# The MLP of the first eight tile rows, done by two between the turns of the second attention half

## The chip, the core and the metric

The kernel runs on one core of a Trainium2 chip. The metric is the device time of one execution in microseconds (us). The core has five engines with a queue each: PE (matrix products), DVE (vector), ACT (activations and copies), POOL (GpSimd) and SP, which here only issues DMAs. In the traces, PEld is the weight load of PE.

## What is computed

Four sequences of 1024 rows with 128 channels go through four residual blocks: sparse attention (16 heads of 8; a row sees the 32 rows up to itself and every 64th row before it), an MLP with weights of +1 and −1, a Mamba block over the sequence, and the same MLP again.

```python
x = x + attention(layernorm(x))            # window 32, stride 64, 16 heads
x = x + ffn(layernorm(x), k0, k1, k2, s0, s1, s2)
x = x + mamba(layernorm(x))
x = x + ffn(layernorm(x), k0, k1, k2, s0, s1, s2)

def ffn(x):                                # 128 -> 512 -> 512 -> 128
    h = concat([x, -x])
    h = relu(s0 * (h @ where(k0, 1, -1))) * 2
    h = relu(s1 * (h @ where(k1, 1, -1))) * 2
    return s2 * (h @ where(k2, 1, -1))
```

## The kernel before

The four sequences are kept as two pairs of batches, `xs[0]` and `xs[1]`, each 128 partitions (2 x 64 rows) by 16 tiles by 128 channels. A tile is thus 64 rows of two sequences at once; a group is four tiles, called by pair and number (0_0 is the first group of the first pair).

**Attention** (`attention`, L201 to L590) runs over 32 tiles, pair 0 then pair 1, in a loop of turns (L546). In turn `i` it does one stage each of several tiles: products of the strided keys for tile `i+1` (`product`, POOL), scores (`scores`, PE) for `i+1`, softmax for `i` (DVE, ACT), weights and strided values for `i-2` (`weights`, `strided`), values for `i-3`, the division for `i-4`, the output projection and the residual for `i-5`. The strided work grows with the tile's number in its pair, on DVE and POOL alike. Beside this, `prep_steps` (L274) norms and projects a group of four tiles, two steps a turn, for groups to come: `xn` (ACT), its transpose `tp` (PE), `xnT`, the products `pq`, `pk`, `pn`, and by DMA on SP the keys `kx` (16 small DMAs a group), and the values out to memory (`vd`) and back (`vr`). ACT spreads `vr` into `vb` (`spread_values`, L477), one quarter a turn. The keys and values of a pair stand in `kv` and `vS` (two buffers each, L270). PE's results of all these steps rotate through five PSUM banks (`spare`, L213).

Within the attention each engine keeps the order in which the program issues its instructions (`keep`, L593); what comes after it in the program is put in order by the scheduler, which may place it between these. The layer norm statistics of the first MLPs stand that way inside the attention on DVE (`st_fa`) and POOL (`rs_fa`) already.

**MLP weights** (L648 to L673): DVE makes `w0`, `w1`, `w2` from the loaded bits after the attention.

**MLP** (`mlp`, L682): for a group of four tiles, norm (`fxna`, ACT), transpose (`ftpa`, PE), split of the transposed values into a high part (ACT) and the rest (`fxnTa`, DVE), first product `pfa` (8 matmuls of 512 columns), relu again as a high part (ACT) and a rest (`h1a`, DVE), second product `pga` (32 matmuls), relu `h2a`, last product `pfoa`, residual on DVE. Work is cut into pieces by generators; two `lanes` (L1186) hold the MLPs of all groups: 0_0 and 0_1 first, then 0_2 and 0_3, and so on. The second lane's first MLP uses buffers of the scans (`in_scan_buffers`, L1180).

**Mamba** needs for its first unit the norm of groups 0_0 and 0_1 (`mamba_norm`, L846; `st_z`, `rs_z`, `mxn`, `mtp`, `mxnT`), then `mamba_pre_half` (L901: convolution `pc`, `px`, `pd`). Until it is ready, a loop (L1204) runs it and the lanes' MLPs by turns. Then `scans` (L1026) works through 128 units, each a pair of scans and a product on DVE (`hs`, `hc`), a product on POOL (`db`) and sums, while the remaining MLPs are fed in by pieces. The last MLPs close the kernel.

Of the kernel before, what the change touches and what calls it, by code (L numbers as in the profile page):

```python
# [16 lines left out]
F32 = mybir.dt.float32  # L17
# [3 lines left out]
F32R = mybir.dt.float32r  # L21
AF = mybir.ActivationFunctionType
ALU = mybir.AluOpType
# [3 lines left out]
P = 128  # L27
B, T, C = 4, 1024, 128
NP = B // 2
R = 64  # L30
NT = T // R
# [4 lines left out]
EPS = 1e-5  # L36
FF = 512
E, N, DC, DR = 256, 16, 4, 8
NH = E // P
CH = 512  # L40
# [3 lines left out]
def hybrid_kernel(ctx: ExitStack, tc: tile.TileContext, x, Wq, Wk, Wv, Wo, ln_g, ln_b, W_in, conv_w,  # L44
# [36 lines left out]
    xs = []  # L81
# [24 lines left out]
    def load_mlp():  # L106
        for t, k in ((k0s, k0), (k1s, k1), (k2s, k2)):
            nc.sync.dma_start(t, k.rearrange("(i p) f -> p i f", p=P))
        for i, s in enumerate((s0, s1, s2, res_scale)):
            nc.sync.dma_start(scal[:, i : i + 1], s.partition_broadcast(P))  # L110
# [87 lines left out]
            )  # L198


    def attention(actx):  # L201


# [68 lines left out]
        prep = {}  # L272

        def prep_steps(cc):  # L274

            bp, c = divmod(cc, NT // 4)
            yield
            xn = ap2.tile([P, 4, C], F32, name=f"xn{cc}", tag="xn")
            rs = norms.pop(cc)
            for i in range(4):  # L280
                sc.activation(
                    xn[:, i, :], xs[bp][:, 4 * c + i, :], AF.Identity, bias=rs[:, 1, i : i + 1],
                    scale=rs[:, 0, i : i + 1],
                )
            yield
            tp = spare(f"tp{cc}")
            for i in range(4):
                te.transpose(tp[:, i * P : (i + 1) * P], xn[:, i, :], ident)
            yield
            xnT = ap2.tile([P, CH], F32, name=f"xnT{cc}", tag="xnT")  # L290
            sc.copy(xnT, tp)
            yield
            pq, pk = spare(f"pq{cc}"), spare(f"pk{cc}")
            te.matmul(pk, wqkv[:, 1, :], xnT, start=True, stop=True)
            te.matmul(pq, wqkv[:, 0, :], xnT, start=True, stop=True)

            def project(i):
                pn = spare(f"pn{cc}_{i}")
                te.matmul(
                    pn[:, : 3 * C], xnT[:, i * P : (i + 1) * P], wqkv.rearrange("p i c -> p (i c)"),  # L300
                    start=True, stop=True,
                )
                return pn

            qs = ap2.tile([P, 4, C], F32, name=f"qs{cc}", tag="qs")

            def keep_rows(i, pn):
                m = 4 * c + i
                sc.copy(qs[:, i], pn[:, :C])
                sc.copy(kv[bp][:, m], pn[:, C : 3 * C])  # L310
                sc.copy(vS[bp][:, :, m], pn[:, 2 * C : 3 * C])

            yield
            kx = kxs[cc % 2]
            qT = ap2.tile([P, CH], F32, name=f"qT{cc}", tag="qT")
            if cc == 0:

                sc.copy(qT, pq)
                for t in range(4):
                    ve.tensor_tensor(  # L320
                        kx[:, t], pk[:, t * P : (t + 1) * P].unsqueeze(1).to_broadcast([P, HB, P]),
                        head_of.unsqueeze(2).to_broadcast([P, HB, P]), ALU.mult,
                    )
            else:
                kT = ap2.tile([P, CH], F32, name=f"kT{cc}", tag="kT")
                sc.copy(kT, pk)
                queues = (nc.sync, nc.gpsimd) if cc == 1 else (nc.sync,)
                for h in range(H):
                    rows = slice(h * HD, (h + 1) * HD)
                    queues[h % len(queues)].dma_start(  # L330
                        kx[rows, :, h % HB, :], kT[rows, :].rearrange("p (t x) -> p t x", t=4)
                    )
                sc.copy(qT, pq)
            prep[cc] = qT, kx
            for i0 in (0, 2):
# [12 lines left out]
            prep[cc] = qT, kx, qs, vr  # L348
# [189 lines left out]
            ve.tensor_add(xs[bp][:, m, :], xs[bp][:, m, :], psum.pop(("y", i))[:, :C])  # L538


        LEAD = 7

        starts = {(3 if cc == 1 else 4 * cc) - LEAD: cc for cc in range(len(tiles) // 4)}
        preps = []
        last = len(tiles)
        for i in range(-LEAD, last + 5):  # L546
            def at(k, stage):
                if 0 <= i + k < last:
                    stage(i + k)

            if i == -LEAD:
                weights_in()
            if i == 0:
# [24 lines left out]
            at(-4, turn_out)  # L578
            at(-3, values)
            at(-4, keep_out)  # L580
            for p in preps:
                next(p, None)
            cc, step = divmod(i + LEAD, 4)
            if cc + 2 < last // 4:
                stats(cc + 2, range(step, step + 1))
                if step == 3:
                    scales(cc + 2)
            cc, step = divmod(i + 1, 4)
            if 0 <= cc < last // 4:
                spread_values(cc, range(step, step + 1))  # L590

    with ExitStack() as actx:
        keep.append(True)  # L593
# [51 lines left out]
                    w.run()  # L645


    fw = ctx.enter_context(tc.tile_pool(name="ffnw", bufs=1))  # L648
    fx = ctx.enter_context(tc.tile_pool(name="ffnx", bufs=2))
    with tc.tile_pool(name="kload", bufs=1) as kl:  # L650


        sign = fw.tile([P, 2], F32, name="sign")
        below = fw.tile([P, 2], F32, name="below")
        ve.tensor_single_scalar(sign, scal[:, 0:2], 0.0, op=ALU.is_gt)
        ve.tensor_single_scalar(below, scal[:, 0:2], 0.0, op=ALU.is_lt)
        ve.tensor_sub(sign, sign, below)
        total = fw.tile([P, 1], F32, name="total")
        ve.tensor_mul(below, scal[:, 0:2], sign)
        ve.tensor_scalar_mul(below, below, 2.0)  # L660
        ve.tensor_mul(total, below[:, 0:1], below[:, 1:2])
        ve.tensor_mul(total, total, scal[:, 2:3])
        twice = fw.tile([P, 2], F32, name="twice")
        ve.tensor_scalar_mul(twice, sign, 2.0)

        w0 = fw.tile([P, FF], F32R, name="w0")
        diff = kl.tile([P, FF], F32, name="diff")
        ve.tensor_sub(diff, k0s[:, 0], k0s[:, 1])
        ve.tensor_scalar_mul(w0, diff, twice[:, 0:1])
        w1 = fw.tile([P, 4, FF], F32R, name="w1")  # L670
        ve.tensor_scalar(w1, k1s, twice[:, 1:2], sign[:, 1:2], ALU.mult, ALU.subtract)
        w2 = fw.tile([P, 4, C], F32R, name="w2")
        ve.tensor_scalar(w2, k2s, 2.0, -1.0, ALU.mult, ALU.add)  # L673
    waste = fw.tile([P, C], F32, name="waste")
    fed = set()

    CT = NT // 4
    HALF = CT // 2
# [501 lines left out]
    def in_scan_buffers(u):  # L1180

        return [m2.tile([P, 2, CH], F32R, name=f"h1{u}_{f}", tag="hc", bufs=6) for f in range(4)]
# [89 lines left out]
```

## Time and profile before

| what | us |
|---|---|
| median of 3 runs (929.16 to 929.56) | 929.18 |
| the profiled execution, whole | 928.12 |
| its span, first to last instruction | 926.3 |
| busy in the span: PE, DVE, POOL, ACT | 753.8, 772.2, 751.3, 588.9 |
| last residual of the attention (DVE) starts | 246.21 |
| first scan (`hs`) starts | 322.55 |

The span is what a trace shows; the difference of 1.8 us to the whole execution lies around it. Shares of busy time are means over very different stages. This is busy time in tenths in 40 slices of 23 us:

```profile
PE   5897578955698879968789988869889969778887
DVE  6799898999623378988799999899999999999952
ACT  4766447743436587788766887877868764754513
POOL 6799996999523287899888999989989998997921
```

The attention fills the first ten slices or so, the scans begin near the fourteenth.

### The profile page before, as it was taken

The page shows a single profiled execution, that of the slowest core. Times are in us where ns is not written, and L with a number is a line of the kernel's source. Part 1 is how long each engine was busy: PE and PEld are TensorE (multiplying, and loading weights), DVE is VectorE, ACT ScalarE, POOL GpSimd, SP SyncE. Part 2 cuts the span into 40 slices and gives each one's busy share as a digit, 9 for nine tenths or more (in the row PEclk, how much of TensorE's full clock was granted, in tenths as well). Part 3 has the DMA queues.
Part 4 walks back from the last instruction along what each step waited for, and adds up shares of the span by engine and source line. Part 5 has one row for each costly group of instructions (what it writes and reads, how often), then busy time and mean ns, then how long its engine had stood idle before and what let it go on. Part 6 is the DMA issues. An engine that isn't in the chain of part 4 may idle for free.

```text
span 926.3 us, 15255 instructions
## 1 busy us (share of the span) xinstructions
PE 753.8 (81%) x5628; PEld 454.6 (49%) x5628; DVE 772.2 (83%) x1033; ACT 588.9 (64%) x1292; POOL 751.3 (81%) x586
## 2 busy tenths in 40 slices
PE   5897578955698879968789988869889969778887
PEld 2454345533486544623346534536435626445556
DVE  6799898999623378988799999899999999999952
ACT  4766447743436587788766887877868764754513
POOL 6799996999523287899888999989989998997921
PEclk9899869996699977997999999999989989799998
DMA  4633313330100121112121121121221221222000
GB/s 134 118 71 68 61 18 69 72 63 2 42 6 1 47 69 47 49 66 67 48 70 46 69 70 47 68 70 46 80 70 46 80 81 46 80 68 73 30 23 12
DMA packets 47162, 53.09 MB, mean 57 GB/s; under 512 B 4824, under 2 KB 38400, under 8 KB 47088
## 3 DMA queue, kind: packets, MB, share of 16 engines
q1 hardware_dynamic: 45920, 51.59, 19.8%
q8 instruction: 44, 0.72, 0.3%
q0 software_dynamic: 608, 0.27, 0.2%
q10 hardware_dynamic: 560, 0.26, 0.1%
q14 instruction: 30, 0.25, 0.1%
HBM read 45.82 MB, written 4.46 MB: 54 GB/s over the span
## 4 chain that ended last, share of the span: by engine, by line
DVE 33%; PE 25%; ACT 16%; POOL 12%; issue 8%; SPq 3%; DMA 3%; DVEq 0%; POOLq 0%; ACTq 0%
DVE hs L57 16%; DVE hc L57 5%; ACT da L57 4%; PE pys L57 4%; PE pga L57 4%; POOL prod L57 3%; DVE S L57 3%; POOL prodv L57 3%; ACT L57 3%; PE pc L57 3%; SPq L330 2%; PE pfoa L57 2%; POOL db L57 2%; PE pd L57 2%; PE pgb L57 2%
## 5 line engine op out<-in xcount | busy, mean ns | idle before, releaser
L57 POOL TENSOR_TENSOR db<-du,bs 128x1024 f32<-128x1024 f32 x128 | 304.0, 2376 | 0.6 <-DMA bs<-bd 0.6
L57 ACT ACTIVATE da<-dt,a_t 128x512 f32<-128x512 f32 x256 | 175.5, 687 | 138.8 <-DVE hs L57 138.2
L57 POOL TENSOR_TENSOR hc<-hc,hc 128x512 f32<-128x512 f32 x128 | 163.9, 1281 | 51.3 <-DVE hc L57 51.3
L57 DVE TENSOR_TENSOR hc<-hs,pcc 128x1024 f32<-128x1024 f32 x128 | 155.9, 1218 | 23.5 <-PE pcc L57 15.6
L57 DVE TENSOR_TENSOR_SCAN hs<-da,db 128x512 f32<-128x512 f32 x128 | 149.0, 1205 | 12.5 <-POOL db L57 6.9
L57 DVE TENSOR_TENSOR_SCAN hs<-da,carry,db 128x512 f32<-128x512 f32 x128 | 156.9, 1266 | 1.9 <-ACT da L57 1.0
L57 PE MATMUL pys<-hc,ident 128*128 128x512 f32 x256 | 144.5, 650 | 0.1
L57 PE MATMUL pcc<-bc,spread 96*128 96x512 bf16 x128 | 52.8, 412 | 36.2 <-DVE hc L57 35.4
L57 PE MATMUL pga<-h1a,w 128*128 128x512 f32 x256 | 74.8, 442 | 8.1 <-ACT u L57 2.9
L57 PEld LDWEIGHTS pys<-hc,ident 128*128 128x128 f32 x256 | 51.7, 211 | 49.7 <-issue 23.6
L57 POOL TENSOR_TENSOR prodv<-vS,E 128x128 f32<-128x128 f32 (+14 forms) x30 | 69.7, 2322 | 5.8 <-ACT E L57 5.5
L57 POOL TENSOR_TENSOR prod<-kv,qs 128x128 f32<-128x128 f32 (+14 forms) x30 | 71.3, 2376 | 1.5 <-DVE or L57 1.4
L57 PEld LDWEIGHTS pga<-h1a,w 128*128 128x128 f32 x256 | 50.8, 202 | 30.7 <-issue 4.8
L57 ACT ACT_TABLE_LOAD x48 | 61.6, 1283 | 3.4 <-issue 2.6
L57 PE MATMUL pc<-mxnT,w_conv 128*128 128x512 f32 x128 | 60.8, 601 | 2.1 <-ACT gate L57 2.1
L57 PE MATMUL pgb<-h1b,w 128*128 128x512 f32 x192 | 56.9, 443 | 5.0 <-DVE h1b L57 3.9
L57 ACT ACTIVATE E<-S 128x512 f32<-128x512 f32 (+15 forms) x62 | 26.5, 473 | 52.4 <-DVE S L57 52.2
L57 PE MATMUL ps<-kx,qT 64*32 64x256 f32 x1008 | 46.5, 438 | 6.4 <-DVE S L57 5.5
L57 PE MATMUL py<-woT,oT 128*128 128x128 f32 x64 | 17.7, 363 | 40.2 <-ACT oT L57 39.9
L57 POOL TENSOR_TENSOR ep<-ep,eo 128x512 f32<-128x512 f32 x32 | 41.2, 1289 | 9.9 <-ACT ep L57 8.6
L57 PEld LDWEIGHTS pgb<-h1b,w 128*128 128x128 f32 x192 | 37.6, 197 | 23.0 <-issue 7.5
L57 ACT COPY ep<-pt 128x512 f32<-128x512 f32 x32 | 18.8, 587 | 38.5 <-DVE eo L57 36.6
(213 smaller groups left out, 1577.0 us busy)
## 6 DMA issues: line engine op xcount, KB each, us to landing
bs<-bd SPq DMA_DIRECT2D x64, 512.0 KB
vr<-vd SPq DMA_DIRECT2D x32, 256.0 KB
vd<-kv SPq DMA_DIRECT2D x8, 256.0 KB
x<-in_L_attn_a_x_dram SPq DMA_DIRECT2D x15, 128.0 KB
kx<-kT SPq DMA_DIRECT2D x104, 16.0 KB
out_dram<-x SPq DMA_DIRECT2D x12, 128.0 KB
taps<-in_L_attn_b_conv_w_dram SPq DMA_DIRECT2D x1, 512.0 KB
k1s<-in_L_ffn_k_dram SPq DMA_DIRECT2D x1, 256.0 KB
```

The source lines that it names most:

```text
L57: ins = getattr(self.engine, name)(*args, **kwargs)
L330: queues[h % len(queues)].dma_start(kx[rows, :, h % HB, :], kT[rows, :].rearrange("p (t x) -> p t x", t=4))
```

## The change

The MLP of groups 0_0 and 0_1 (eight tiles) leaves the lanes. A new generator `mlp_first` does it by two tiles, 256 columns at a time, in the attention's turns 17 and after; four calls of `other()` a turn advance it by one step each. It takes a buffer of `kv` and one of `vS`, those of pair 0, which are no longer needed then. Its PSUM banks come from `spare` too. The weights are made by `mlp_weights`, in turns 12 to 15, in parts. To make room for the weights, which now stand beside the attention's buffers, `xn`, `xnT` and `vr` have one buffer instead of two; `vr` is loaded two turns later and spread to `vb` by two quarters in a turn, two turns later; group 1's preparation starts one turn later. The scan buffers are no longer lent to the second lane.

```diff
+    def mlp_weights():
...
+        ve.tensor_single_scalar(sign, scal[:, 0:2], 0.0, op=ALU.is_gt)
...
+        yield
+        ve.tensor_sub(w0, k0s[:, 0], k0s[:, 1])
+        ve.tensor_scalar_mul(w0, w0.bitcast(F32), twice[:, 0:1])
+        ve.tensor_scalar(w2, k2s, 2.0, -1.0, ALU.mult, ALU.add)
+        for i in range(2):
+            yield
+            part = slice(2 * i, 2 * i + 2)
+            ve.tensor_scalar(w1[:, part], k1s[:, part], twice[:, 1:2], sign[:, 1:2], ALU.mult, ALU.subtract)
...
-            xn = ap2.tile([P, 4, C], F32, name=f"xn{cc}", tag="xn")
+            xn = ap2.tile([P, 4, C], F32, name=f"xn{cc}", tag="xn", bufs=1)
...
-            xnT = ap2.tile([P, CH], F32, name=f"xnT{cc}", tag="xnT")
+            xnT = ap2.tile([P, CH], F32, name=f"xnT{cc}", tag="xnT", bufs=1)
...
-            vr = ap2.tile([P, 16, C], F32, name=f"vr{cc}", tag="vr")
+            prep[cc] = qT, kx, qs
+            for _ in range(4):
+                yield
+            vr = ap2.tile([P, 16, C], F32, name=f"vr{cc}", tag="vr", bufs=1)
...
+        def mlp_first(nt):
+            cols = 2 * C
+            room = ap2.tile([P, NT * 2 * C], F32R, name="roomk", tag="kv")
+            rest = ap2.tile([P, C * NT], F32, name="roomv", tag="vS")
...
+            for t in range(nt):
+                if t % 2 == 0:
+                    yield
+                st = small.tile([P, 6], F32, tag="sta", name=f"stm{t}", bufs=2)
+                ve.bn_stats(st, xs[0][:, t, :])
+                ve.bn_aggr(mv[:, t, :], st)
+            yield
...
+            gp.tensor_tensor(rs[:, 0], rs[:, 0], minus_half[:, :nt], ALU.pow)
...
+            for t0 in range(0, nt, 2):
+                yield
+                for k in range(2):
...
+                    sc.activation(
+                        xn[:, k * C : (k + 1) * C], xs[0][:, t, :], AF.Identity, bias=rs[:, 1, t : t + 1],
+                        scale=rs[:, 0, t : t + 1],
+                    )
+                yield
+                tp = spare(f"mt{t0}")[:, :cols]
+                for k in range(2):
+                    te.transpose(tp[:, k * C : (k + 1) * C], xn[:, k * C : (k + 1) * C], ident)
+                yield
+                sc.copy(xnT[:, 0], tp)
+                yield
+                ve.tensor_sub(xnT[:, 1], tp, xnT[:, 0].bitcast(F32))
+                for f0 in (0, 2):
+                    yield
+                    pf = spare(f"mf{t0}_{f0}").rearrange("p (f c) -> p f c", f=2)
+                    for f in range(2):
+                        for s in range(2):
+                            te.matmul(
+                                pf[:, f], w0[:, (f0 + f) * P : (f0 + f + 1) * P], xnT[:, s], start=s == 0, stop=s == 1
+                            )
+                    yield
+                    sc.activation(h1[:, f0 : f0 + 2, 0], pf, AF.Relu)
+                    yield
+                    ve.scalar_tensor_tensor(
+                        h1[:, f0 : f0 + 2, 1], pf, 0.0, h1[:, f0 : f0 + 2, 0].bitcast(F32), ALU.max, ALU.subtract
+                    )
+                for f0 in (0, 2):
+                    yield
+                    pg = spare(f"mg{t0}_{f0}")
+                    for f in range(2):
+                        for j in range(4):
+                            for s in range(2):
+                                te.matmul(
+                                    pg[:, f * cols : (f + 1) * cols], w1[:, j, (f0 + f) * P : (f0 + f + 1) * P],
+                                    h1[:, j, s], start=j + s == 0, stop=j == 3 and s == 1,
+                                )
+                    yield
+                    sc.activation(h2[:, f0 * cols : (f0 + 2) * cols], pg, AF.Relu)
+                yield
+                po = spare(f"mo{t0}")[:, :cols]
...
+                yield
+                xc = xs[0][:, t0 : t0 + 2, :].rearrange("p m c -> p (m c)")
+                ve.scalar_tensor_tensor(xc, po, total, xc, ALU.mult, ALU.add)
...
-        starts = {(3 if cc == 1 else 4 * cc) - LEAD: cc for cc in range(len(tiles) // 4)}
+        starts = {4 * cc - LEAD: cc for cc in range(len(tiles) // 4)}
+        weights_made = mlp_weights()
+        beside = mlp_first(2 * NT // 4)
...
+            if NT - 4 <= i < NT:
+                next(weights_made, None)
+            def other():
+                if i > NT:
+                    next(beside, None)
...
             at(-2, weights_before)
+            other()
...
                 at(1, keep_scores)
+            other()
             at(0, softmax_scores)
             at(0, softmax_exp)
+            other()
...
             for p in preps:
                 next(p, None)
+            other()
...
-            cc, step = divmod(i + 1, 4)
-            if 0 <= cc < last // 4:
-                spread_values(cc, range(step, step + 1))
+            cc, step = divmod(i - 1, 4)
+            if 0 <= cc < last // 4 and step < 2:
+                spread_values(cc, range(2 * step, 2 * step + 2))
...
-    fed = set()
+    fed = {("a", 0, 0), ("a", 0, 1)}
...
-            early(0, lane, f1, lane, *[in_scan_buffers] * lane),
             early(0, 2 + lane, f1, lane),
```

On PE the new order in four turns of one pair of tiles is: transposes (`mt`) at the end of the first, then `mf` after the scores of the second and of the third, `mg` twice in the fourth (one before `py`, one after the scores), and `mo` in the next turn before `py`.

More of the change, by code (lines that the diff above doesn't have):

```diff
@@ L198, in ln_apply @@
             )
+    fw = ctx.enter_context(tc.tile_pool(name="ffnw", bufs=1))
+    w0 = fw.tile([P, FF], F32R, name="w0")
+    w1 = fw.tile([P, 4, FF], F32R, name="w1")
+    w2 = fw.tile([P, 4, C], F32R, name="w2")
+    total = fw.tile([P, 1], F32, name="total")
+    def mlp_weights():
+        sign = small.tile([P, 2], F32, name="sign", tag="sign", bufs=1)
+        below = small.tile([P, 2], F32, name="below", tag="below", bufs=1)
+        twice = small.tile([P, 2], F32, name="twice", tag="twice", bufs=1)
+        ve.tensor_single_scalar(sign, scal[:, 0:2], 0.0, op=ALU.is_gt)
+        ve.tensor_single_scalar(below, scal[:, 0:2], 0.0, op=ALU.is_lt)
+        ve.tensor_sub(sign, sign, below)
+        ve.tensor_mul(below, scal[:, 0:2], sign)
+        ve.tensor_scalar_mul(below, below, 2.0)
+        ve.tensor_mul(total, below[:, 0:1], below[:, 1:2])
+        ve.tensor_mul(total, total, scal[:, 2:3])
+        ve.tensor_scalar_mul(twice, sign, 2.0)
+        yield
[6 more added lines that the diff above has]
+            ve.tensor_scalar(w1[:, part], k1s[:, part], twice[:, 1:2], sign[:, 1:2], ALU.mult, ALU.subtract)
     def attention(actx):
@@ L538, in residual @@
             ve.tensor_add(xs[bp][:, m, :], xs[bp][:, m, :], psum.pop(("y", i))[:, :C])
+        def mlp_first(nt):
+            cols = 2 * C
+            room = ap2.tile([P, NT * 2 * C], F32R, name="roomk", tag="kv")
+            rest = ap2.tile([P, C * NT], F32, name="roomv", tag="vS")
+            h1 = room[:, : 8 * cols].rearrange("p (f s c) -> p f s c", f=4, s=2)
+            xnT = room[:, 8 * cols : 10 * cols].rearrange("p (s c) -> p s c", s=2)
+            h2, xn = rest[:, : 4 * cols], rest[:, 4 * cols : 5 * cols]
+            mv = small.tile([P, nt, 2], F32, name="mvm", tag="mvm", bufs=1)
+            for t in range(nt):
[5 more added lines that the diff above has]
+            yield
+            rs = small.tile([P, 2, nt], F32, name="rsm", tag="rsm", bufs=1)
+            gp.tensor_scalar_add(rs[:, 0], mv[:, :, 1], EPS)
+            gp.tensor_tensor(rs[:, 0], rs[:, 0], minus_half[:, :nt], ALU.pow)
+            gp.tensor_scalar_mul(rs[:, 1], mv[:, :, 0], -1.0)
+            gp.tensor_mul(rs[:, 1], rs[:, 1], rs[:, 0])
+            for t0 in range(0, nt, 2):
+                yield
+                for k in range(2):
+                    t = t0 + k
+                    sc.activation(
[38 more added lines that the diff above has]
+                po = spare(f"mo{t0}")[:, :cols]
+                for k in range(2):
+                    for f in range(4):
+                        te.matmul(
+                            po[:, k * C : (k + 1) * C], h2[:, f * cols + k * C : f * cols + (k + 1) * C],
+                            w2[:, f].bitcast(F32), start=f == 0, stop=f == 3,
+                        )
+                yield
+                xc = xs[0][:, t0 : t0 + 2, :].rearrange("p m c -> p (m c)")
+                ve.scalar_tensor_tensor(xc, po, total, xc, ALU.mult, ALU.add)
@@ L587, in attention @@
                     scales(cc + 2)
-            cc, step = divmod(i + 1, 4)
-            if 0 <= cc < last // 4:
-                spread_values(cc, range(step, step + 1))
+            cc, step = divmod(i - 1, 4)
+            if 0 <= cc < last // 4 and step < 2:
+                spread_values(cc, range(2 * step, 2 * step + 2))
+        for g in (weights_made, beside):
+            for _ in g:
+                pass
     with ExitStack() as actx:
@@ L645, in weave @@
                     w.run()
-    fw = ctx.enter_context(tc.tile_pool(name="ffnw", bufs=1))
     fx = ctx.enter_context(tc.tile_pool(name="ffnx", bufs=2))
[L650 to L674, printed above, removed]
-    fed = set()
+    waste = fx.tile([P, C], F32, name="waste", bufs=1)
+    fed = {("a", 0, 0), ("a", 0, 1)}
     CT = NT // 4
@@ L1178, in hybrid_kernel @@
     m2 = work.enter_context(tc.tile_pool(name="mam2", bufs=2))
-    def in_scan_buffers(u):
-        return [m2.tile([P, 2, CH], F32R, name=f"h1{u}_{f}", tag="hc", bufs=6) for f in range(4)]
     first_half = range(HALF)
```

## The prediction

> **What bounds the kernel now.** I read the page's 40 slices first, then busy time by stage, then the chain of waits over the stretch between attention and scans, then busy time turn by turn in the second half of the attention. Four stages come out: attention on the first pair of batches (up to 129.3 us), attention on the second pair (to 246.2), a stretch that gets the first scan going (to 322.5), and the scans with their tail.
>
> ```profile
> core 0: us, PE busy (x) PEld busy (x) DVE busy (x) ACT busy (x) POOL busy (x), PEclk, DMA share, GB/s
> 0.00:129.30 129.30, 93.13 (x1558) 55.49 (x1558) 108.37 (x241) 74.84 (x195) 112.42 (x108) 0.91 0.39 83
> 129.30:246.20 116.90, 86.04 (x1886) 57.29 (x1886) 104.88 (x188) 58.44 (x151) 100.90 (x63) 0.84 0.22 43
> 246.20:322.50 76.30, 67.48 (x294) 48.39 (x295) 27.69 (x66) 43.24 (x86) 22.20 (x35) 0.91 0.11 29
> 322.50:926.30 603.80, 507.13 (x1892) 293.44 (x1890) 531.24 (x538) 412.42 (x862) 515.73 (x382) 0.91 0.18 58
> ```
>
> In the third stage PE works 67.5 of 76.3 us while DVE and POOL, the two busiest engines of all other stages, rest for two thirds of it. The chain of waits says what PE does there (start, length, what):
>
> ```profile
> 255.38 3.75 PE pfa L57 x10
> 259.13 15.36 PE pga L57 x64
> 274.49 5.37 PE pfoa L57 x48
> ...
> 285.36 0.50 ACT mxn L57
> ...
> 298.57 6.87 PE pc L57 x16
> ...
> 316.07 3.95 DMA bs<-bd
> 320.15 2.36 POOL db L57
> 322.55 1.22 DVE hs L57
> ```
>
> From 255.38 to 285.90 (the first mtp transpose) the end waits for the MLP of groups 0_0 and 0_1 and for the norm behind it. Then come one more MLP (0_2), the convolution pc and the first scan.
>
> The second attention half, by turns (19, 20, 22, 24, 28 and 30; a turn begins at its DVE COPY_PREDICATED):
>
> ```profile
> 148.75:153.10 4.35, 3.64 (x41) 1.97 (x40) 4.32 (x12) 3.19 (x7) 4.02 (x4) 1.00 1.13 207
> 153.10:158.65 5.55, 5.55 (x137) 3.79 (x138) 4.75 (x13) 3.48 (x8) 3.86 (x4) 1.00 0.24 41
> 163.50:169.20 5.70, 5.39 (x153) 3.65 (x142) 5.20 (x12) 5.49 (x17) 5.15 (x4) 1.00 0.26 66
> 174.70:180.50 5.80, 5.76 (x172) 3.94 (x157) 5.70 (x11) 3.54 (x8) 5.55 (x4) 1.00 0.29 48
> 199.80:206.90 7.10, 3.35 (x105) 2.37 (x105) 7.00 (x12) 2.63 (x6) 7.10 (x4) 1.00 0.01 2
> 214.30:222.00 7.70, 4.85 (x105) 2.99 (x105) 7.60 (x12) 2.76 (x6) 7.70 (x3) 0.78 0.01 2
> ```
>
> Up to turn 25 PE is nearly full, since keys and values of later tiles are projected there too; after that PE has room, but DVE and POOL have none.
>
> [...] an MLP matmul whose operand is late holds the attention's transposes behind it; the trace agrees in so far as PE's waits (py for oT, 1.4 to 3.7 us a turn) hold everything after them. [...] the granted clock falls to 0.50 at 228 to 233 us and to 0.75 in turn 27[...]. [...]
>
> **The change, part by part.** In the order of instructions of the two kernels, everything from the first pcc, hs, da and db on is the same on PE, DVE, ACT and POOL. So the sum is the shift of the first scan, now at 322.5.
>
> *Removed after the attention.* In the new order, PE goes from the attention's last py (its residual at 246.2) through the transposes straight to pfa of group 0_2. In front of it stay fxna, spread, w_conv with its loads and the low half of fxnTa, as now: 9.2 us (246.2 to 255.38). Behind it stays 285.90 to 322.55, 36.6 us. What goes is 285.90 − 255.38 = 30.5 us. The weights' DVE work (247.3 to 250.6) also goes, but w_conv then waits for taps, now third in SP's queue behind w_in and w_out: I count nothing either way, −2 to +3. Gain 30.5, bounds 28 to 33.
>
> *Prices of the moved work.* The last stage has the same shapes:
>
> ```profile
> L57 PE MATMUL pgc<-h1c,w 128*128 128x256 f32 x64 | 8.0, 286 | 0.0
> L57 DVE SCALAR_TENSOR_TENSOR ox<-pfoc,total,ox 128x256 f32<-128x256 f32 x2 | 1.0, 484 | 10.0 <-PE pfoc L57 10.0
> L57 DVE TENSOR_TENSOR fxnTc<-ftpc,fxnTc 128x256 fp32r<-128x256 f32 x2 | 0.8, 424 | 4.2 <-ACT fxnTc L57 4.2
> ```
>
> 64 matmuls of 256 columns fill 8.0 us, 0.125 each. [...] A pair of tiles: mf 8 × 0.125 = 1.0; mg 32 × 0.125 = 4.0; mo 16 records at 7.30/64 = 0.114, 1.8; mt 0.3: 7.1 us PE, 28.5 for four pairs. DVE: sub 0.42, two low halves of 0.68 (h1a row), the add 0.48: 2.3 a pair. Its statistics cost 8 × 0.46 = 3.7 (st_fa rows, 0.28 + 0.17), and the mamba norm's st_z, hoisted in too, 0.44 a tile. ACT gets some 3.5 a pair against 58.4 busy of 116.9: hidden.
>
> *First half, to 129.3.* Out: st_fa of eight tiles, 3.7 us DVE, and two rs_fa on POOL, 1.7 each. In: the weights, 4.2 DVE in turns 12 to 15, where DVE already waits for POOL 3.1, 1.1 and 0.6 us. The single buffers xn, xnT and vr, the later vr load and the vb copies two by two: each buffer's last reader stands a turn before its next writer, so no wait; two copies in one ACT turn cost 0.6 where ACT has 40% free. SP keeps vd, vr, then kx; chunk 1's kx goes a turn later, but the second tile's scores stand earlier on PE and ACT, no longer behind a vb that waited 2.6 us for its DMA. I take −3 (−5 to 0).
>
> *Turns 17 and 18.* Eight statistics, 3.7, against DVE idle 12.45 − 10.02 = 2.4: +2 (1 to 4).
>
> *Turns 19 to 25.* PE is busy 34.5 of 37.9 us, 3.3 free. Pair 0 brings mf, mg, mo (6.8), pair 1 mt, mf, mg (5.3): 12.1 − 3.3 = 8.8. The five rotating banks now serve eight tiles in a turn with mg and projections; the next pt then waits for ACT's h2, behind four norm activations (1.65): +1.7 for both such places. 10.5 (8 to 16).
>
> *Turns 26 to 31.* DVE has 0.1 a turn. Pair 1's add, pair 2 whole, pair 3's sub and four st_z: 0.5 + 2.3 + 0.4 + 1.8 = 5.0. POOL's rs_z (3 × 0.22 + 1.67 + 0.2 + 0.24 = 2.8) runs beside it, mg in PE's holes. +5 (3.5 to 8).
>
> *Turns 32 to 36.* Pair 3's low halves 1.4; a hoisted rs_fa of 1.7 ahead of POOL's last prodv, which is on the chain; mg and mo, 5.8, partly in PE's waits. +3.5 (1.5 to 7).
>
> Slip of the attention: −3 + 2 + 10.5 + 5 + 3.5 = +18. Net 18 − 30.5 = −12.5: span 926.3 to 913.8. The profiled run took 928.12 and the median is 929.18; I shift the median: 916.7.
>
> **Rivals.** (1) The holes are better than counted: PE clock nearer 1.0, the lag of turns 19 to 25 caught up in PE's free 2 to 3 us of turns 26 to 31. Slip 9, the sum of the low ends: 929.2 − 21.5 = 907.7. For it: PE's own idle from 186 us on exceeds what is added. Against: DVE and POOL are at 98 to 100% there. (2) Slower: PE's queue. The four slots a turn put mf behind the DVE sub of the same turn, mg behind its low half, mo behind ACT. There are 24 such groups; if each stops PE for 0.8 us with the attention's pa and pt behind it, that is 19 more, slip 37, 936 us. It decides from a mean extra stop of (30.5 − 18)/24 = 0.5 us. For it: turns 19 to 25 leave PE no slack to catch up. Against: each operand is made a quarter turn ahead, and in turns 26 to 31 PE waits anyway. (3) The earlier scan start is given back: the scans' rate is DVE's and POOL's (531 and 516 busy of 604), but if the first units stop for something with its own time, the end stays at 929. Against: every later instruction depends on the scan's own order, and its only DMA, bs, is made after the start.
>
> **Numbers.** Forecast 0.60, rival 1 0.20, rival 2 0.14, rival 3 0.06. Predicted 916.7. The range 906 to 930 holds the first two and the near side of the third. Within 0.2% (1.9 us, what a measurement of this kernel can tell from no change) falls 0.04; faster 0.82; slower 0.14.
>
> **What would show it.** Right: the last attention residual near 264 us, first hs near 310, the distance between them near 46 (now 76), and the scans still 604 long. Turns 19 to 25 longer by some 10 us with PE full, 26 to 31 by 5 with DVE full. Wrong: PE idle before mf or mg in most turns (rival 2), a distance clearly over 46, or scans longer than 604 (rival 3).

## The result, and the profile after

| | before | after |
|---|---|---|
| median, us (4 runs each, on one chip) | 929.17 | 936.04 (935.88 to 936.24) |
| ratio | | 1.0089, interval [1.0073, 1.0106] |
| span of the profiled execution | 926.3 | 934.1 |
| last residual of the attention | 246.21 | 284.58 |
| first scan `hs` | 322.55 | 334.04 |

The change makes the kernel slower by 0.9%; forecast was 1.3% faster. The attention ends 38.4 us later (forecast 18), the stretch behind it is 26.9 us shorter (forecast 30.5), the scans 3.7 us shorter. 38.4 − 26.9 − 3.7 = 7.8, the difference of the spans.

Busy time by stage in the changed kernel, with the same four stages as in the prediction (first attention half, second half, stretch, scans and tail):

```profile
core 0: us, PE busy (x) PEld busy (x) DVE busy (x) ACT busy (x) POOL busy (x), PEclk, DMA share, GB/s
0.00:137.00 137.00, 94.68 (x1558) 55.10 (x1558) 117.59 (x238) 74.68 (x195) 111.21 (x101) 0.90 0.37 78
137.00:284.60 147.60, 115.17 (x2118) 87.47 (x2118) 119.49 (x246) 71.52 (x180) 108.75 (x80) 0.85 0.17 34
284.60:334.00 49.40, 42.30 (x142) 26.45 (x143) 13.73 (x18) 30.41 (x60) 19.26 (x22) 0.79 0.16 44
334.00:934.10 600.10, 503.31 (x1892) 291.51 (x1890) 531.02 (x538) 412.08 (x862) 514.03 (x382) 0.92 0.17 59
```

The first half has become 7.7 us longer although not one matmul was added to it: PE has the same 1558, DVE's busy time went from 108.4 to 117.6. The second half has 29 us more of PE and 14.6 more of DVE. PE is idle for 32.4 us there, as before for 30.9: the MLP did not fill PE's holes, its time came on top of them.

From here on a turn is measured from its maximum on DVE (`mx<-S`) to the next turn's. The lag of the changed kernel at these maxima grows as follows: 2.4 us at turn 11, 10.4 at turn 13, 7.7 at turn 17, 13.3 at turn 19, 29.8 at turn 26, 35.4 at turn 31, 38.4 at the last residual. Four of the turns of the second half, 18, 21, 25 and 28:

```profile
155.65:165.05 9.40, 6.47 (x113) 4.74 (x113) 5.32 (x15) 5.96 (x14) 6.63 (x8) 0.68 0.07 20
178.79:189.41 10.62, 8.97 (x147) 7.45 (x148) 5.78 (x13) 7.50 (x20) 6.17 (x4) 1.00 0.12 32
212.23:221.16 8.93, 8.74 (x204) 7.00 (x202) 7.04 (x12) 5.72 (x16) 8.11 (x5) 1.00 0.12 34
237.41:246.89 9.48, 6.57 (x63) 5.51 (x62) 7.94 (x12) 3.21 (x7) 9.48 (x5) 0.82 0.01 3
```

They took 6.12, 5.15, 6.40 and 7.36 us before. DVE, which filled 98% of turns 25 and 28 before, is busy for 79 and 84% of them now. It stands and waits. What it waits for, in the changed kernel, from the maximum of turn 17 to the last residual (us in total, times, longest):

```profile
DVE rden L57 <- PE pa L57: 8.8, 7, 2.6
DVE roomk L57 <- ACT roomk L57: 6.7, 7, 1.4
DVE x L57 <- PE py L57: 5.3, 5, 2.6
DVE eo L57 <- PE pt L57: 4.5, 3, 3.1
```

and in the kernel before, over the same turns:

```profile
DVE rden L57 <- PE pa L57: 2.3, 2, 1.6
DVE S L57 <- ACT S L57: 2.1, 2, 1.7
DVE or L57 <- POOL prodv L57: 2.1, 2, 1.7
DVE x L57 <- PE py L57: 1.0, 1, 1.0
DVE S L57 <- POOL prod L57: 0.8, 1, 0.8
```

This gives a balance. The stretch of turns takes 104.4 us before and 135.1 after, 30.7 more. DVE's busy time in it went from 93.2 to 107.2, +14.0. Its waits for PE went from 3.3 to 18.6, +15.3; for ACT from 2.1 to 6.7, +4.6; for POOL from 2.9 to 0. Together 31.0. So both DVE's own new work and its new waits for PE are in the longer turns, one after the other. The balance alone doesn't show which engine sets the pace: busy and idle time of any engine add up to the stretch (PE: 75.9 busy and 28.5 idle before, 105.4 and 29.8 after).

The first half is another matter. This is turn 11 in the changed kernel on DVE and on POOL (start, length, what):

```profile
92.98 1.46 DVE L57 TENSOR_SCALAR sign<-scal 128x2 f32<-128x2 f32 x1
94.35 1.31 DVE L57 TENSOR_SCALAR below<-scal 128x2 f32<-128x2 f32 x1
95.69 2.98 DVE L57 TENSOR_TENSOR sign<-sign,below 128x2 f32<-128x2 f32 x1
...
90.94 3.48 POOL L57 TENSOR_TENSOR prod<-kv,qs 128x1536 f32<-128x1536 f32 x1
94.33 1.30 POOL L57 TENSOR_TENSOR ep<-ep,eo 128x512 f32<-128x512 f32 x1
95.55 3.11 POOL L57 TENSOR_TENSOR prodv<-vS,E 128x1408 f32<-128x1408 f32 x1
```

Three operations on two elements a partition take 5.8 us; behind the attention, in the kernel before, they took 0.17, 0.16 and 0.15. Each ends when the POOL operation under way ends: 94.44 against 94.42, 95.66 against 95.63, 98.67 against 98.66. The time is shown as busy, not as a wait. Such a stretch is called a hold from here on. The ends agree to 0.03 us; what makes the one operation last until the other ends, no trace shows. The attention's own DVE operations (reductions, or one input from PSUM) ran beside POOL's in the kernel before without such stretches: between 30 and 246 us none of their forms varies by more than 0.07 us.

### The profile page after: what moved, and what is told of

It reads as the page before. It is cut to its first block, busy times and chain, and to the rows that moved or that the text cites. A ratio compares the mean times of both kernels' runs of the same rounds, so it can differ in the third digit from the quotient of the medians.

```text
span 934.1 us, 15415 instructions
## 1 busy us (share of the span) xinstructions
PE 755.5 (81%) x5708; PEld 460.5 (49%) x5708; DVE 781.8 (84%) x1038; ACT 588.7 (63%) x1294; POOL 753.2 (81%) x582
## 4 chain that ended last, share of the span: by engine, by line
DVE 40%; PE 28%; ACT 18%; POOL 7%; issue 6%; DMA 1%; SPq 0%; DVEq 0%; POOLq 0%; ACTq 0%
DVE hs L57 15%; DVE S L57 6%; ACT da L57 5%; DVE hc L57 4%; PE pys L57 4%; ACT L57 3%; PE pc L57 3%; DVE or L57 3%; PE pga L57 3%; DVE mx L57 2%; ACT waste L57 2%; POOL db L57 1%; PE pgc L57 1%; PE mg L57 1%; PE pgb L57 1%
## 5 line engine op out<-in xcount | busy, mean ns | idle before, releaser
L57 DVE TENSOR_TENSOR hc<-hs,pcc 128x1024 f32<-128x1024 f32 x128 | 155.9, 1218 | 20.1 <-PE pcc L57 12.1
L57 POOL TENSOR_TENSOR prodv<-vS,E 128x128 f32<-128x128 f32 (+14 forms) x30 | 69.4, 2314 | 18.4 <-ACT E L57 15.3
L57 POOL TENSOR_TENSOR prod<-kv,qs 128x128 f32<-128x128 f32 (+14 forms) x30 | 71.2, 2372 | 10.5 <-DVE or L57 10.3
L57 PEld LDWEIGHTS pys<-hc,ident 128*128 128x128 f32 x256 | 51.0, 208 | 49.9 <-issue 24.8
L57 PE MATMUL pga<-h1a,w 128*128 128x512 f32 x192 | 62.0, 470 | 10.8 <-ACT h1a L57 3.2
L57 PE MATMUL ps<-kx,qT 64*32 64x256 f32 x1008 | 47.1, 458 | 15.6 <-DVE S L57 13.1
L57 PEld LDWEIGHTS pga<-h1a,w 128*128 128x128 f32 x192 | 40.3, 215 | 31.1 <-issue 5.0
L57 POOL TENSOR_TENSOR du<-dt,u 128x512 f32<-128x512 f32 x16 | 20.8, 1300 | 28.3 <-ACT dt L57 28.3
```

The lines of the kernel that those rows point to most:

```text
L57: ins = getattr(self.engine, name)(*args, **kwargs)
```

## The experiments

Two theories stand behind them: that the first half lost its time to these holds (the hold theory: a small DVE operation lasts until the POOL operation under way ends; the first forecast of each of the first three runs is its), and that PE's order in the second half holds up what DVE needs. Rivals are that the added work costs what it costs wherever it stands. The runs were made on four chips, each ratio against the kernel before on the same chip. There the time of one kernel varied by some 0.7% from execution to execution (the kernel before: 924.3 to 931.7), so stretches inside the traces are compared first, and totals only by their intervals. The traces scatter too. Turns 0 to 4 differ by some 3.5 us between traces of the changed kernel's code and by 2.2 between two of the kernel before's; what is said of the first half is counted from turn 11 on, unless said otherwise. From turn 17 to the last residual, four traces with the same code there take 134.3 to 137.2 us: a difference of 1 or 2 us in this stretch shows nothing by itself.

**The small operations on POOL.** The eight operations of sign, below, total and twice:

```diff
-        ve.tensor_single_scalar(sign, scal[:, 0:2], 0.0, op=ALU.is_gt)
+        gp.tensor_single_scalar(sign, scal[:, 0:2], 0.0, op=ALU.is_gt)
...
```

> Only the eight small operations of the weights (sign, below, total, twice) go from DVE to POOL; w0, w1, w2 stay on DVE in the same turns. [...] turns 11 and 12, now 6.4 and 1.5 us longer than before, lose 4 to 6 of these 7.9, of which turn 13's gain of 3.2 may be given back; the time falls from 936.0 to about 932 (929.5 to 933.5). Rival (what costs is the weights' work itself, wherever it runs, in turns where POOL is full): POOL gets some 8 x 0.23 = 1.8 us more, turns 11 to 13 keep their sum, 935.5 to 937.

Ratio to before 1.0102 [1.0058, 1.0145]: the expected gain isn't there, and the median, 936.3, is the one that the rival gave. Turn 11 is healed, 7.43 us, but turn 12 takes 13.80 instead of 9.32:

```profile
103.72 3.73 DVE L57 TENSOR_SCALAR w<-w,twice 128x512 fp32r<-128x512 f32 x1
107.37 1.48 DVE L57 TENSOR_SCALAR w<-k2s 128x512 fp32r<-128x512 uint8 x1
...
103.02 4.14 POOL L57 TENSOR_TENSOR prod<-kv,qs 128x1664 f32<-128x1664 f32 x1
107.13 1.44 POOL L57 TENSOR_TENSOR ep<-ep,eo 128x512 f32<-128x512 f32 x1
```

In the changed kernel the two DVE operations took 0.49 and 0.42: POOL was late there from the holds of turn 11 and ran small operations for a norm, `rsa` (128x4), beside them. These held nothing: `w<-k2s` takes 0.42 beside an `rsa` of 1.25 us, as it did beside an idle POOL behind the attention in the kernel before. So the cost moved to two other operations of the weights, which met POOL's large ones: they end 0.29 and 0.28 us after `prod` and `ep`. Turns 11 to 15 lag by 3.95 us instead of 5.29. POOL's eight took 0.2 each, as expected.

**Three small operations alone.** In the kernel before, at the head of turn 12's instructions:

```diff
+            if i == NT - 4:
+                ve.tensor_single_scalar(sign, scal[:, 0:2], 0.0, op=ALU.is_gt)
+                ve.tensor_single_scalar(below, scal[:, 0:2], 0.0, op=ALU.is_lt)
+                ve.tensor_sub(sign, sign, below)
```

> The kernel before, and in turn 12 at its head three DVE operations of 128x2 (sign, below, sign minus below; nothing reads them), as the changed kernel has them there. [...] each is held until a POOL operation ends, together 3 to 6 us, and the last residual of the attention comes 2 to 5 us later; time 931 to 934. Rival (sum of durations): 3 x 0.16 = 0.5 us, most of it hidden in DVE's wait for POOL in that turn; 929.0 to 929.7.

The hold by itself:

```profile
92.74 3.09 DVE L57 TENSOR_SCALAR sign<-scal 128x2 f32<-128x2 f32 x1
95.75 1.31 DVE L57 TENSOR_SCALAR below<-scal 128x2 f32<-128x2 f32 x1
97.09 2.98 DVE L57 TENSOR_TENSOR sign<-sign,below 128x2 f32<-128x2 f32 x1
...
92.35 3.46 POOL L57 TENSOR_TENSOR prod<-kv,qs 128x1536 f32<-128x1536 f32 x1
95.74 1.29 POOL L57 TENSOR_TENSOR ep<-ep,eo 128x512 f32<-128x512 f32 x1
96.96 3.10 POOL L57 TENSOR_TENSOR prodv<-vS,E 128x1408 f32<-128x1408 f32 x1
```

7.4 us for three operations; the turn takes 14.75 instead of 7.49. Of these 7.3, 4.4 come back in turn 13, where DVE had waited 3.1 us for POOL's `prodv` in the kernel before; a DVE that is late needn't wait. Net 2.55 us at turn 16, within the expected 2 to 5. The time, ratio 1.0016 [0.9998, 1.0034], doesn't settle it; the trace does.

**The weights in turns 2 to 5.**

```diff
-            if NT - 4 <= i < NT:
+            if 2 <= i < 6:
```

> The changed kernel with the same weight work, the same engines, in turns 2 to 5 instead of 12 to 15. [...] POOL's operations are 0.5 to 1.5 us there and POOL has holes, so the weights cost 1 to 3 us instead of 5.3, and turn 13 is as long as in the kernel before (12.6 us); the attention's first half ends 2 to 4 us earlier. Rival (4.2 us of DVE work cost what they are wherever DVE is full, as it is in turns 2 to 5): 4 us there and no gain.

The holds are there too, but POOL's operations of these early turns are short (the products run over few keys yet), 0.5 to 1.6 us:

```profile
31.97 0.59 DVE L57 TENSOR_SCALAR sign<-scal 128x2 f32<-128x2 f32 x1
...
33.01 0.92 DVE L57 TENSOR_TENSOR below<-scal,sign 128x2 f32<-128x2 f32 x1
...
44.07 0.78 DVE L57 TENSOR_SCALAR w<-k1s,twice,sign 128x1024 fp32r<-128x1024 uint8 x1
```

The eight small operations are done in 2.6 us instead of 6.6, and a half of w1 takes 0.78 here against 1.27 among POOL's large operations. Turn 11 is 7.43 again, and from turn 11 to turn 16 the kernel gains 3.6 us on the kernel before, where the changed one loses 5.3: 8.9 us by a move alone, of the weights' work and of its holds together. What the weights cost in turns 2 to 5 has to be set against it. Counted from the start of the kernel, four traces with the early weights lag by 0.5 to 1.7 us at turn 17, and nine with the late ones by 6.5 to 10.3: some 7 us are gained, far more than the scatter. Turn 13 was expected at 12.6, but takes 9.02: in the kernel before POOL makes rs_fa of group 0_0 there, 1.8 us ahead of `prodv`, and the change took that away. The ratio to before is 1.0019 [1.0001, 1.0038], where the changed kernel had 1.0089. The hold theory stands.

**PE's wait before the transposes.** PE waits 12.0 us in four places at `mt` for ACT's norm. First a slot more before `mt` and before `mo`:

```diff
+                yield
                 tp = spare(f"mt{t0}")[:, :cols]
...
+                yield
                 po = spare(f"mo{t0}")[:, :cols]
```

> The changed kernel, with one slot more between the norm xn and its transposes mt, and one more between the last h2 and mo, so that PE meets both operands a quarter turn later. Queue theory (PE stops in order before mt and mo, with the attention's pt and py behind): the waits mt<-ACT and mo<-ACT, 8 and 1.7 us in the trace, nearly go, and the attention ends 5 to 8 us earlier; time 928 to 931. Rival (the slip is the sum of PE's and DVE's added work): it only moves the same work; 934.5 to 937.

The wait stays, 10.7 us: the first norm waits for POOL's `rsm`, and the later ones then stand behind an `ep` or `E` that waits for DVE. From turn 17 to the last residual it takes 29.4 us more than before (30.7 without the slots): 1.3, not 5 to 8. Ratio 1.0057 [1.0002, 1.0112]. Then, with every slot kept, the norms of the second to fourth pair issued five slots, a turn and a quarter, earlier:

```diff
                     sc.activation(h2[:, f0 * cols : (f0 + 2) * cols], pg, AF.Relu)
+                    if f0 == 0 and t0 + 2 < nt:
+                        norm(t0 + 2)
```

> The changed kernel; the norms xn of the second, third and fourth pair of tiles are issued on ACT with the first h2 of the pair before, two turns earlier; no other slot moves. Queue theory (PE stands at mt because the norm is queued on ACT behind an E or ep that waits for DVE): the three long waits of mt for ACT (1.99, 3.15 and part of the rest, of 12.0 in all) go, and the attention from turn 17 on takes 4 to 6 us less than the 30.6 us that it has over the kernel before. Rival (PE's, DVE's and POOL's added work alone): 0 to 1 us less; what PE doesn't wait at mt it waits at pt or pa.

PE's waits in the changed kernel:

```profile
PE mt L57 <- ACT roomv L57: 12.0, 4, 3.9
PE py L57 <- ACT oT L57: 4.3, 4, 1.7
```

and with the norms early:

```profile
PE py L57 <- ACT oT L57: 10.4, 7, 2.9
PE mf L57 <- ACT roomk L57: 4.1, 3, 3.2
PE mt L57 <- ACT roomv L57: 3.9, 1, 3.9
```

8.1 us of PE's wait go, 6.1 come back at `py`, which needs something from DVE's round, and 2.7 at `mf`. The turns are 29.4 us over before: 1.3 gained, which is within the scatter and far from 4 to 6. Ratio 1.0083 [1.0052, 1.0114]. The rival's forecast (0 to 1) was nearer. PE's largest wait wasn't what the turns waited for.

**PE's work.** The low halves of h1 left out of mg (so h2 is made from the high halves alone):

```diff
-                            for s in range(2):
-                                te.matmul(... h1[:, j, s], start=j + s == 0, stop=j == 3 and s == 1)
+                            te.matmul(... h1[:, j, 0], start=j == 0, stop=j == 3)
```

> The changed kernel, with the low halves of h1 left out of mg in the attention: 64 matmuls of 256 columns less, 64 x 0.125 = 8.0 us of PE; DVE, ACT and the order stay. Rival (PE's added work is the bound): the attention ends 7 to 8 us earlier, 928 to 929. Queue theory (late operands, not PE's work, hold the turns): only mg's share in turns without a hole counts, 2 to 4 us earlier, 932 to 934.

26.8 us over before: 3.9 gained for 8.0 us of PE, as the queue theory had it, though the scatter leaves this uncertain by some 1.5 us. DVE's waits for PE fall from 18.6 to 16.0. So part of PE's time is paid for, but not all of it. Ratio 1.0077 [1.0056, 1.0098].

**DVE's work.** The same, and the DVE operations that make the low halves left out too:

> The changed kernel without the low halves of h1 in the attention: their products are left out of mg (64 matmuls, 8.0 us of PE) and the DVE operations that make them too (8 x 0.69 = 5.5 us); the slots stay. The run without the products alone took 26.8 us more than the kernel before from turn 17 to the last residual (30.7 with all). Sum of both engines (DVE paces the turns; its added work and its added waits for PE and ACT both lengthen them): 5.5 us of work and 2 to 4 us of DVE's waits for ACT's relu go, 17.5 to 20. Rival (PE's added time alone sets the turns): 26 to 27, as DVE's work lies beside it.

24.4 us over before, between both forecasts. In the turns up to 31 it is 6.3 us less than without the products alone (19.15 against 25.45 of lag since turn 17), so DVE's work and its waits for ACT's relu do count there; the tail, from there to the last residual, then takes 22.3 us instead of 18.5, with DVE waiting 3.6 for POOL's last `prodv`, which the hoisted rs_fa precedes. The step from 26.8 to 24.4 is no larger than the scatter. Ratio 1.0057 [1.0042, 1.0071].

**One and two slots later.**

```diff
+            for _ in range(1):
+                yield
             cols = 2 * C
```

> The changed kernel; the whole MLP of the eight tiles begins one slot later, so that every step sits one slot on: mg stands behind the scores ps and behind the values pa, mo behind ps, instead of ahead of py and of pn, and mt behind pt. In-series theory ([...] a piece ahead of py and ps delays the residual and scores that DVE meets next, so the MLP's PE time is added to the turns although PE idles 28 us there): the attention from turn 17 to its last residual, 30.7 us more than before, comes down to 23 to 27. Sum rival (the added busy time of PE decides, 29.5 us, wherever it stands): 30 to 32.

> The changed kernel with the MLP two slots later: mg ahead of pn and ahead of py again (third and first slot), mo in the third. In-series theory: as in the changed kernel, 27 to 31 us from turn 17 on, clearly more than with one slot. Sum rival: 30 to 32, the same as with one slot.

27.7 and 28.4 us over before. One slot misses its 23 to 27, and two slots aren't clearly worse than one; nor do the totals gain, with ratios of 1.0083 [1.0051, 1.0114] and 1.0114 [1.0073, 1.0155]. Both are a little better than the changed kernel and alike, which speaks against mg's place before py or pn: with two slots mg stands there again. Much of it is only displaced: at turn 31 the lag since turn 17 is 20.1 and 19.9 (27.7 in the changed kernel), but the tail then adds 7.6 and 8.5 instead of 3.0. What the first arrangement had worse isn't settled; mo ahead of py (in turn 21 DVE waits 2.6 us for py behind it) may be a part, and wasn't tried alone.

**The load of a_t.** Issued first of the loads on POOL's queue:

```diff
+    a_t = mw.tile([P, NH, N], F32, name="a_t")
+    nc.gpsimd.dma_start(a_t, A_log.rearrange("(h p) n -> p h n", p=P))
     g_t, b_t = vec("ln_g", ln_g, 1), vec("ln_b", ln_b, 1)
```

> The changed kernel; of the loads on POOL's queue behind the attention, that of a_t is issued first instead of tenth. Theory (of the 3.4 us by which the stretch from the last residual to the first hs exceeds the forecast 46, most is the exponential of a_t, which ACT meets ahead of h1 and which waits 5.0 us for its load): the stretch falls from 49.5 to 46 to 47.5 us, with nothing changed before it. Rival (w_conv behind taps, or the granted clock, makes the 3.4 us): it stays at 49 to 50.

The stretch is 48.5 us instead of 49.5: missed, by the rival too. Ratio 1.0104 [1.0057, 1.0150]. The exponential moved to the head of ACT's order with its load, and now ACT waits 3.9 us there, with PE's last `ftpa` behind it (4.2). This, the early norms and the early weights were then put together:

> The changed kernel with all three edits: norms early, the load of a_t first, weights in turns 2 to 5. If the three causes are separate, the gains add: 5 + 2.5 + 3 = 10.5 us less than the changed kernel, about 925.5 on its scale of 936.0, some 3.5 under the kernel before; ratio to before 0.994 to 0.998. If they overlap (a wait that goes opens the next), 930 to 934, ratio 1.001 to 1.005.

It gave no more than the weights alone: ratio 1.0040 [1.0025, 1.0055], stretch 48.9 us.

**One slot later, weights in turns 2 to 5, a_t at turn 0.** The load of a_t beside those of the MLP's weights, its exponential where it was:

```diff
             nc.sync.dma_start(scal[:, i : i + 1], s.partition_broadcast(P))
+        nc.sync.dma_start(a_t, A_log.rearrange("(h p) n -> p h n", p=P))
```

> One slot later, the weights in turns 2 to 5, and a_t loaded with the MLP's weights at turn 0, so that ACT meets its exponential with the data there. Against the changed kernel's span of 934.1: first half -6.4 (as with the weights alone), slots -4 to -7, stretch from 49.5 to 46 -3: about 919, ratio to before 0.990 to 0.996. If the slots give nothing: 924.5, ratio 0.997 to 1.000. If a_t isn't what holds the stretch it stays at 49.

Its first three stages:

```profile
0.00:129.80 129.80, 96.56 (x1556) 56.29 (x1556) 112.35 (x238) 74.27 (x195) 108.92 (x100) 0.88 0.39 82
129.80:271.50 141.70, 110.05 (x2120) 83.21 (x2120) 120.34 (x247) 71.60 (x182) 110.53 (x81) 0.90 0.19 36
271.50:316.30 44.80, 40.88 (x142) 25.99 (x143) 13.55 (x17) 30.22 (x59) 18.50 (x21) 0.85 0.16 48
```

This one beats both kernels, but by little: ratio to before 0.9966 [0.9952, 0.9980], where 0.990 to 0.996 was expected. The span of 919.0 is that of one of its fastest executions (920.8 us; the median of 20 is 923.2). The first half is as long as before's, the second 25 us longer, the stretch 31.5 us shorter. The second half's 24.8 us over before are 2.9 less than with one slot alone, by the same code: scatter. In the changed kernel the stretch had this (DVE, POOL, POOL's issue, ACT, PE):

```profile
285.35 2.29 DVE L57 TENSOR_TENSOR spread<-spread_ids 128x2048 bf16<-128x2048 int32 x1 [0.47 <-issue]
285.39 2.31 POOL L57 TENSOR_TENSOR rs_z<-rs_z 128x8 f32<-128x8 f32 x1
...
295.69 0.76 POOL L915 DMA_DIRECT2D a_t<-in_L_attn_b_A_log_dram  x1
...
297.79 0.23 ACT L57 ACTIVATE a_t<-a_t 128x32 f32<-128x32 f32 x1 [5.01 <-DMA a_t<-in_L_attn_b_A_log_dram]
297.93 2.04 ACT L57 ACTIVATE h1a<-pfa 128x512 fp32r<-128x512 f32 x4
298.56 2.80 PE L57 MATMUL pga<-h1a,w 128*128 128x512 f32 x5 [2.95 <-ACT h1a L57]
```

With a_t loaded early:

```profile
280.74 2.06 ACT L57 ACTIVATE h1a<-pfa 128x512 fp32r<-128x512 f32 x4 [1.08 <-PE pfa L57]
281.78 2.41 PE L57 MATMUL pga<-h1a,w 128*128 128x512 f32 x5
```

From the last residual pga comes after 10.3 us instead of 14.0. POOL's queue issues a_t's load last of eleven, and starts on them only after rs_z, which itself is held by DVE's `spread` (2.31 us for an operation that took 0.20 before). The run with a slot more agrees, with a_t's load still last: there the loads stood ahead of rs_z on POOL, ACT waited 1.2 us for a_t instead of 5.0, pga came after 10.8 us and the stretch took 46.1.

**Four tiles only, late.**

```diff
-        beside = mlp_first(2 * NT // 4)
+        beside = mlp_first(NT // 4)
...
-                if i > NT:
+                if i > NT + 8:
...
+            *(early(0, 1, f1, lane) for _ in range(lane)),
             early(0, 2 + lane, f1, lane),
```

> Only group 0_0 (four tiles, two pairs) is done in the attention, from turn 25 on, where keys and values are all made; group 0_1 is done behind the attention by a lane; weights in turns 2 to 5, a_t early. It adds 6.4 us of DVE and 14.2 of PE to turns in which PE has 2 to 3 us free. In-series theory: the attention from turn 17 on takes 11 to 14 us more than in the kernel before, the stretch behind it 76.3 - 15 = 61, total 921 to 924 on before's span of 926.3. Rival (DVE's added work alone counts, PE's lies in its holes): 6 to 8 us more, total 914 to 917.

15.2 us over before, a little more than the in-series theory's 11 to 14 and twice the rival's 6 to 8, with 15.5 us of PE and 7.9 of DVE added, and DVE's waits for PE at 9.4 (3.3 before). But the total, expected to gain, is the worst of all, ratio 1.0157 [1.0129, 1.0185]. The stretch didn't shrink: 76.7 us, with 128 matmuls of pga in it (112 in the kernel before). The other lane no longer had a group of the first half to do and ran MLPs of later groups, which nothing at the start of the scans needs, through the same PE. My edit left that lane free.

## Why the prediction was wrong

The forecast span was 913.8, the measured 934.1: 20.3 us off. By its own terms, in which a turn begins at its COPY_PREDICATED, half a turn or more ahead of the maximum used so far:

**First half, −3: measured +7.7, 10.7 off.** The failed step is "In: the weights, 4.2 DVE in turns 12 to 15, where DVE already waits for POOL", counted as free. I took the durations of these operations from behind the attention, where POOL was idle, and moved them to a place where POOL is hardly ever idle (it is busy for 37.4 of the 38.0 us from 90.5 to 128.5 in the kernel before), and I read a wait for POOL as room. They took 10.8 us there instead of 4.2. That POOL holds them is shown by the three operations alone (7.3 us in one turn, 2.55 net) and by the move to turns 2 to 5 (8.9 us back in turns 11 to 15). The rest of the term holds: with the weights gone turns 11 to 15 gain 3.6 us from the removed statistics and rs_fa. The 2.4 us of lag at turn 11 aren't explained. They are within the scatter of turns 0 to 4; single buffers and the vb copies two by two may have a part in them, and that wasn't tried.

**Turns 17 and 18, +2: measured +0.6.** DVE's idle time took most of the statistics up.

**Turns 19 to 25, +10.5: measured +18.9**, the largest miss and above the stated 16. In the kernel before and in the changed one:

```profile
148.75:186.63 37.88, 34.54 (x750) 22.25 (x748) 36.14 (x74) 26.95 (x70) 34.84 (x25) 1.00 0.41 77
157.03:213.86 56.83, 46.44 (x842) 34.59 (x843) 41.25 (x86) 32.62 (x82) 38.22 (x30) 0.92 0.27 53
```

The failed step is "12.1 − 3.3 = 8.8". PE's new work was sized rightly, 11.9 us. But the 3.3 us of free time could not be subtracted: PE stands idle for 10.4 us there now, 6.5 of them before `mt` and `mo`. And DVE's new work, 5.1 us, was counted at nothing, though DVE had only 1.7 us idle; it has 15.6 now. PE's idle time wasn't free: 2.6 of the 3.3 us were a wait for oT, which comes from DVE's `o` by way of PE and ACT. That each engine waits longer for the other when both have more to do fits this, but isn't tested by itself. Taking work away shortened the turns from 17 on by less than that work (3.9 us for 8.0 of PE, then 2.4 for 5.5 of DVE), and taking most of PE's largest wait away did not shorten them clearly. In the balance above the second half's 30.7 are 14.0 of DVE work and 17.0 of DVE's waits; I had counted the greater engine of each group of turns, not both. How the 17.0 divide among the causes of single waits isn't shown. One is known: PE's 2.9 us before the first `mt`, for which the norm waits on POOL's rsm, were not in the sum.

**Turns 26 to 31, +5, and 32 to 36, +3.5: measured +11.1 together.** This is within the stated ranges. 6.8 us of it are DVE's new work, the rest its waits.

**The stretch, −30.5: −26.9.** The failed step is that only `w_conv` was seen as coming under a load. It was a_t, last on POOL's queue, whose exponential stands on ACT ahead of h1 (5.0 us of waiting). The MLP that was taken away had covered most of that load (1.05 us of waiting before). With the load early the stretch lost 31.5 us, so the term came out, though not by its own sum: pga starts 10.3 us after the last residual, where the sum has 12.9 (259.13 − 246.21), and the rest takes 1.7 us longer.

**Scans unchanged: 3.7 us shorter.** Over all 15 traces the part from the first hs to the end takes 598.7 to 603.8 us, and 601.9 in the run with three signs, whose scans are those of before; so half of it at least is scatter. Rival 3, by which the gain would be given back there, did not come.

**The rivals.** Rival 1's better clock didn't come: PE was granted 0.85 in both kernels from turn 17 to the last residual (0.92 instead of 1.00 in turns 19 to 25, 0.81 instead of 0.74 after them). Rival 2 names the time, 936, and the slip, 37 (measured 38.4), but that is luck. Its 40 us for turns 17 to 36 (21 of the forecast and 19 more) were 30.7, and its gain of 3 in the first half was a loss of 7.7. Its mechanism is PE stopping before the MLP's groups, and PE does stop there for 18.8 us (mt 12.0, mg 2.8, mo 2.6, mf 1.4), as it reckoned; but when 8.1 of these were taken away, 1.3 came out. The holds no rival had.

Two more figures on PE. The weight loads of 128 columns (PEld) take 194 ns on average in `pgc` and 210 in `mg`, where the prediction counts 125 ns for a matmul of 256 columns; what they add to the matmuls isn't shown. And rival 1's clock nearer 1.0 from work in PE's idle time isn't shown: 0.50 was granted from 224 to 235 us in the kernel before, where PE's longest idle time since 214 us is 2.9 us, and 1.00 from 199.8 to 206.9 us, where PE is busy for 3.35 of 7.10 us.

## What to carry to other kernels

A duration holds for the neighbours it was measured beside: before a DVE operation is moved among POOL's, look in a trace how long its like takes beside a busy POOL (three of 0.15 to 0.17 us took 7.4 us here), and put it where POOL's operations are short. An engine's idle time inside a cycle of engines is not room; ask which engine paces the cycle, and add its own new work and its new waits. When work is taken from in front of a stage, list every load whose landing it had covered, in the order of its queue.

## What the runs showed of the hardware

Three DVE operations of 128x2, 0.15 to 0.17 us each beside an idle POOL, took 3.09, 1.31 and 2.98 us beside a busy one. The hold can last longer than one of POOL's operations: in the run with a_t's load first, `sign` alone took 5.73 us and the two behind it 0.15 and 0.16, while the longest of POOL's operations beside the three in the changed kernel, `prod`, takes 3.48. Not every operation of POOL holds: beside `rsa` (128x4, 1.25 us) `w<-k2s` took 0.42 us, as beside an idle POOL. It works the other way too: POOL's operation of 128x8 on rs_z took 2.31 us instead of 0.20 while DVE made `spread` (2.29 us, two inputs in SBUF), and ended 0.06 us after it. Neither shows as a wait in the profile, only as a duration out of line for its size.
